# Householder QR in front of a transformer block: the column products move from VectorE to TensorE, one matmul per row chunk

## The chip, the cores and the metric

One Trainium2 chip, one of its cores. The metric is the device time of one launch in microseconds (us). The core's engines are called by the profile's names: PE is TensorE (PEld its weight loads), DVE is VectorE, ACT is ScalarE, POOL is GpSimd, SP issues DMAs. Each engine works through its own queue in order; they meet only at semaphores. Everything is float32.

## The reference, cut to what matters

The input `x` is 8 x 512 x 576, `cond` is 8 x 576. First the tokens are rotated inside a 64-dimensional subspace, and then a transformer block with modulation from `cond` runs over them:

```python
U, _ = jnp.linalg.qr(P)                       # P is 576 x 64
R = expm(skew(silu(cond) @ W.T + b))          # 8 rotations, 64 x 64
z = jnp.einsum('btn,nd->btd', x, U)
x = x + jnp.einsum('btd,nd->btn', einsum('btd,bde->bte', z, R) - z, U)
ada = silu(cond) @ ada_w + ada_b              # shift, scale, gate, twice
x = x + gate_msa * attention(modulate(layernorm(x)))   # per token, 16 x 16 over heads
x = x + gate_mlp * mlp(modulate(layernorm(x)))
```

The QR factorisation is needed before the first token can be rotated, and it is the part that is changed.

## The kernel before, in words

**Two stages.** The first 241 us hold the preparation: the QR, the exponentials and the modulation. From there to the end PE works through the transformer block for 8 batches in 16 units of 256 tokens (qkv, projection, fc1, fc2), while DVE does the attention of a later unit. The block begins with the rotation of the first 128 tokens, which needs the finished QR and the finished exponential of batch 0.

**The QR.** `m` holds P as five chunks of 128 rows (the last half empty): `[128, 5, 64]`. `qr_step(j)` is called for j = 0..63 in order; each step needs what the step before wrote to `m`. In the kernel before, one step with n = 64 - j columns left does this:

- DVE multiplies all chunks by column j (`pr`, L263) and adds the five chunks up (`t`, L268). From 16 columns on, both go in two halves of the columns. `column_products` does it at the end of the step before.
- PE fetches row j of `m` to all partitions (`rp`, L274, the weights are one column of the identity spread over 128 columns) and adds `t` over the partitions (`dp`, L282, the weights are ones). `dp[:, j]` is the squared norm, `dp[:, j+1:]` the products of column j with the others.
- DVE takes the sign (`sg`, L291), clears entry j of the column (L292), makes the signed row (`row`, L295); ACT takes the root (`nrm`, L298) and the negated sign (`nsg`, L299).
- DVE makes `w` (L320), `den` (L323), its reciprocal `r` (L335), the outer product (`up`, L327, two halves) and adds it to `m` with `r` (L337, two halves).
- `av`, `vmax`, `dg` (L306 to L310) and the write of the diagonal entry (L311, by `done`, in the next step) stand behind the products of the next column.

**The side work.** After each step from j = 2 on, one piece of `beside()` is put into the queues: the 40 matmuls that make the skew entries (L405), the nine column groups of `ada` (L364, five matmuls each, 128 x 8 weights, 384 columns), four modulation pieces (L375, weights 8 x 128) and the matrix exponential: products of 64 x 64 (L429, eight per product, 16 instructions), 13 pieces ahead of 19 squarings. A squaring makes two products (`pe`, `pf`), each copied by ACT and raised by POOL before the next squaring. `paced(4, ...)` lets four skew matmuls through per step, `paced(3, ...)` three modulation pieces, the latter also beside the first 13 pieces of the exponential. So j = 4 to 13 have skew matmuls, j = 14 to 30 `ada` and the start of the exponential, j = 31 to 49 the squarings, and j = 50 to 63 next to nothing.

**What sets the order.** PE, DVE, ACT and POOL carry their instructions in the order of the program here (a hand-written schedule); only the SP queue is ordered by the scheduler. So the order in which the loop calls `qr_step` and `beside` is the order of the queues. A float32 matmul is two LDWEIGHTS and two MATMUL instructions on PE; the profile counts both.

**After the loop** the diagonal entry of the last column is written (`done`), `vv` = the products of all columns (L577) gives the triangular inverse in some 30 us of small matmuls, and the rotation of the first tokens follows.

Of the kernel before, what the change touches and what calls it, by code (L numbers as in the profile page):

```python
# [18 lines left out]
R = 64  # L19
# [4 lines left out]
NK = len(KROWS)  # L24
# [25 lines left out]
def rotate_then_dit_block(  # L50
# [18 lines left out]
    nc = tc.nc  # L69
# [21 lines left out]
    ident = const.tile([128, 128], F32, tag="ident", name="ident")  # L91
# [23 lines left out]
    small = ctx.enter_context(tc.tile_pool(name="small", bufs=4))  # L115
# [48 lines left out]
    with tc.manual_schedule(engines=engines), tc.tile_pool(name="prep", bufs=1) as prep, tc.tile_pool(name="qrs", bufs=2) as qrs, tc.tile_pool(  # L164
        name="ada", bufs=4
    ) as adap, tc.tile_pool(name="exs", bufs=1) as exs, tc.tile_pool(
        name="ps_qr", bufs=1, space=PSUM
    ) as ps_qr, tc.tile_pool(
        name="ps_ex", bufs=2, space=PSUM
    ) as ps_ex, tc.tile_pool(name="ps_m", bufs=2, space=PSUM) as ps_m, tc.tile_pool(  # L170
        name="ps_x", bufs=1, space=PSUM
    ) as ps_x:
        m = prep.tile([128, NK, R], F32, tag="m", name="m")
# [12 lines left out]
        ones = prep.tile([128, 128], F32, tag="ones", name="ones")  # L186
# [56 lines left out]

        vmax = prep.tile([128, R], F32, tag="vmax", name="vmax")

        def halves(lo):
            n = R - lo
            if n < 16:  # L250
                return [(lo, R)]
            return [(lo, lo + n // 2), (lo + n // 2, R)]

        def wide(n):
            return [128, NK, n]

        def column_products(j):

            t = qrs.tile([128, R], F32, tag="t", name=f"t_{j}")
            prods = []  # L260
            for h, (a, b) in enumerate(halves(j)):
                pr = qrs.tile(wide(R), F32, tag=f"pr{h}", name=f"pr_{j}_{h}", bufs=1)
                nc.vector.tensor_tensor(  # L263
                    pr[:, :, a:b], m[:, :, a:b], m[:, :, j : j + 1].to_broadcast(wide(b - a)), ALU.mult
                )
                prods.append(pr)
            for pr, (a, b) in zip(prods, halves(j)):
                nc.vector.tensor_reduce(t[:, a:b], pr[:, :, a:b].rearrange("p c i -> p i c"), AX.X, ALU.add)  # L268
            return t

        def qr_step(j, t, done):

            rp = ps_qr.tile([128, R], F32, tag="rp", name=f"rp_{j}")
            nc.tensor.matmul(  # L274
                rp[:, j:R],
                lhsT=ident[:, j : j + 1].to_broadcast([128, 128]),
                rhs=m[:, 0, j:R],
                start=True,
                stop=True,
            )  # L280
            dp = ps_qr.tile([128, R], F32, tag="dp", name=f"dp_{j}")
            nc.tensor.matmul(dp[:, j:R], lhsT=ones, rhs=t[:, j:R], start=True, stop=True)  # L282

            def small(tag):
                return qrs.tile([128, 1], F32, tag=tag, name=f"{tag}_{j}")

            n = R - j
            row, sg, nsg, nrm, av = (small(x) if x != "row" else None for x in ("row", "sg", "nsg", "nrm", "av"))
            row = qrs.tile([128, R], F32, tag="row", name=f"row_{j}")

            nc.vector.tensor_scalar(sg, rp[:, j : j + 1], 0.0, -2.0, ALU.is_ge, ALU.mult)  # L291
            nc.vector.tensor_tensor(  # L292
                m[:, 0, j:R], m[:, 0, j:R], off[:, j : j + 1].to_broadcast([128, n]), ALU.mult
            )
            nc.vector.scalar_tensor_tensor(  # L295
                row[:, j:R], sg.to_broadcast([128, n]), 1.0, rp[:, j:R], ALU.add, ALU.mult
            )
            nc.scalar.activation(nrm, dp[:, j : j + 1], AF.Sqrt, bias=tiny)  # L298
            nc.scalar.activation(nsg, sg, AF.Identity, bias=ones[:, 0:1])  # L299
            if done:  # L300
                done()

            def finish():

                dg = small("dg")
                nc.vector.tensor_scalar(av, nrm, row[:, j : j + 1], None, ALU.subtract)  # L306
                nc.vector.tensor_reduce(
                    vmax[:, j : j + 1], m[:, :, j], AX.X, ALU.max, apply_absolute_value=True
                )
                nc.vector.tensor_scalar(dg, ident[:, j : j + 1], av, nsg, ALU.mult, ALU.mult)  # L310
                return lambda: nc.vector.tensor_tensor(  # L311
                    m[:, 0, j : j + 1], m[:, 0, j : j + 1], dg, ALU.subtract
                )

            if j + 1 == R:
                return None, finish()

            w = qrs.tile([128, R], F32, tag="w", name=f"w_{j}")
            den, r = small("den"), small("r")
            nc.vector.scalar_tensor_tensor(  # L320
                w[:, j + 1 : R], row[:, j + 1 : R], nrm, dp[:, j + 1 : R], ALU.mult, ALU.subtract
            )
            nc.vector.tensor_scalar(den, nrm, row[:, j : j + 1], nrm, ALU.subtract, ALU.mult)  # L323
            outer = []
            for h, (a, b) in enumerate(halves(j + 1)):
                up = qrs.tile(wide(R), F32, tag=f"up{h}", name=f"up_{j}_{h}", bufs=1)
                nc.vector.tensor_tensor(  # L327
                    up[:, :, a:b],
                    m[:, :, j : j + 1].to_broadcast(wide(b - a)),
                    w[:, a:b].unsqueeze(1).to_broadcast(wide(b - a)),  # L330
                    ALU.mult,
                )
                outer.append(up)
                if h == 0:
                    nc.vector.reciprocal(r, den)  # L335
            for up, (a, b) in zip(outer, halves(j + 1)):
                nc.vector.scalar_tensor_tensor(  # L337
                    m[:, :, a:b], up[:, :, a:b], r, m[:, :, a:b], ALU.mult, ALU.add
                )
            return column_products(j + 1), finish()  # L340

        def paced(n, parts):

            k = 0
            for part in parts:
                for _ in part:
                    k += 1
                    if k % n == 0:
                        yield
# [49 lines left out]
        def skew_entries(g):  # L399

            ps = ps_m.tile([B, GROUP], F32, tag="m", name=f"skew_{g}")
            cols = slice(g * GROUP, (g + 1) * GROUP)
            for c in range(NK):
                k = srows(c)
                nc.tensor.matmul(ps, lhsT=sc[0:k, c, :], rhs=wr[0:k, c, cols], start=c == 0, stop=c == NK - 1)  # L405
                yield
            nc.scalar.mul(skew[:, 1 + g * GROUP : 1 + (g + 1) * GROUP], ps, 2.0**-N_SQUARINGS)
# [109 lines left out]
        def modulations():  # L517

            for g in range(9):
                yield from ada_columns(g)  # L520
                if g + 4 < 9:
                    load_ada(g + 4)
                v = {1: 0, 2: 1, 5: 3, 7: 4}.get(g)
                if v is not None:
                    modulation(v)
                    yield

        def beside():
            yield
            yield  # L530
            yield from paced(4, [skew_entries(g) for g in range(8)])
            skew_rows()
            rest = paced(3, [modulations()])
            for _ in range(4):
                next(rest)
                yield
            for free in expm(*eyes):
                if free:
                    next(rest, None)
                yield  # L540
# [10 lines left out]
        first_xt = xin.tile([128, D], F32, tag="xt", name="xt_0_0", bufs=2)  # L551
        eyes = identities()
        side = beside()
        t, done = column_products(0), None
        for j in range(R):
            t, done = qr_step(j, t, done)
            if j > 1:
                next(side, None)
            if j == 30:
                nc.sync.dma_start(out=first_xT, in_=x_t[0, :, :, 0:256].rearrange("c p s -> p c s"))  # L560
                nc.sync.dma_start(out=first_xt, in_=x[0, 0:128, :])
            if j == 8:
                load_rows(wqkv, qkv_w, 65)
                nc.sync.dma_start(out=b1, in_=fc1_b)
# [4 lines left out]


        if True:
            done()
# [108 lines left out]
            for n in range(2):  # L681
                cols = slice(n * HALF, (n + 1) * HALF)
# [10 lines left out]
            for n in range(2):  # L693
# [513 lines left out]
    for k, (b, ts) in enumerate(units):  # L1207
# [5 lines left out]
        pr = Projection(b, ts, gate_a)  # L1213
# [89 lines left out]
```

## Time and profile before

| | us |
|---|---|
| median of three runs | 2156.08 (2156.01 to 2163.45) |
| profiled execution, its own time | 2157.38 |
| its span, first to last instruction | 2155.7 |
| QR, first `rp` to the end of the last `dp` | 4.51 to 209.42 |
| triangular inverse and first rotation | 209.4 to about 241 |
| transformer block | 241 to the end |

The 64 steps in five stretches, by the starts of `rp` in the trace:

| steps | side work | from, to (us) | us | us per step |
|---|---|---|---|---|
| j = 0 to 3 | none | 4.51 to 20.70 | 16.2 | 4.0 |
| j = 4 to 13 | skew | 20.70 to 56.92 | 36.2 | 3.6 |
| j = 14 to 30 | `ada`, start of the exponential | 56.92 to 119.89 | 63.0 | 3.7 |
| j = 31 to 49 | squarings | 119.89 to 176.91 | 57.0 | 3.0 |
| j = 50 to 63 | next to none | 176.91 to 209.42 | 32.5 | 2.3 |

How to read the lines that are quoted further on: a line of the timeline has the start, the time from the first start to the last end, the engine, the line of the kernel, the operation, the tiles (out<-in), shapes and how many instructions were merged (x2 is one float32 matmul). `128*8` is the shape of the weights. The view by windows gives, for a stretch of time, the busy time and the count of instructions of each engine, and PEclk, the share of its full clock that PE was granted. A busy time over the whole window is cut at the window's length.

### The profile page before, as it was taken

How to read it: one execution, taken by the hardware profiler on the slowest of the kernel's cores; microseconds unless marked ns; L12 is line 12 of the kernel's file. 1: busy time of each engine (PE TensorE's matmuls, PEld its weight loads, DVE VectorE, ACT ScalarE, POOL GpSimd, SP SyncE). 2: the span in 40 equal slices, each digit the busy share in tenths (PEclk: the TensorE clock that was granted, in tenths of full speed). 3: DMA queues.
4: the chain of work that ended last, by engine and by line, in shares of the span. 5: the costliest groups of instructions: out<-in, count | busy, mean ns of one | idle time of the engine just before them, and what ended most of it. 6: DMA issues, size and time to landing. Idle time of an engine off the chain costs nothing.

```text
span 2155.7 us, 28203 instructions
## 1 busy us (share of the span) xinstructions
PE 2052.0 (95%) x10091; PEld 1622.7 (75%) x10091; DVE 1818.0 (84%) x2544; ACT 433.6 (20%) x1040; POOL 731.8 (34%) x959
## 2 busy tenths in 40 slices
PE   6996998999999999999999999999999999999988
PEld 3475666777878888787878787888878778787867
DVE  8998499799997988979797979797988998986920
ACT  2232121212111111221121212111221121112110
POOL 2341143241523333333333242423333443343422
PEclk9965799999999999999999999999999999999989
DMA  8202265385857666565758484857667666665744
GB/s 278 87 2 75 85 209 164 114 234 161 225 178 223 194 191 222 174 217 178 234 143 271 133 266 127 244 176 210 213 180 234 187 210 182 200 189 193 218 129 131
DMA packets 251456, 392.44 MB, mean 182 GB/s; under 512 B 86926, under 2 KB 139099, under 8 KB 251316
## 3 DMA queue, kind: packets, MB, share of 16 engines
q1 hardware_dynamic: 225396, 364.09, 55.3%
q10 hardware_dynamic: 25920, 26.55, 3.6%
q8 instruction: 80, 1.31, 0.2%
q14 instruction: 60, 0.49, 0.1%
HBM read 331.63 MB, written 58.94 MB: 181 GB/s over the span
## 4 chain that ended last, share of the span: by engine, by line
PE 77%; DVE 12%; issue 3%; DMA 3%; POOL 3%; ACT 1%; ACTq 0%; SPq 0%; POOLq 0%; DVEq 0%
PE fc L993 25%; PE qkvp L821 17%; PE fc L1067 9%; PE pj L949 6%; PE fc L1072 6%; PE p L1097 3%; PE fc L1069 3%; DVE sc L866 2%; DVE qk L859 1%; DVE pv L887 1%; PE zps L751 1%; DVE att L894 1%; PE rot L762 1%; PE dp L282 1%; PE htr L794 1%
## 5 line engine op out<-in xcount | busy, mean ns | idle before, releaser
L993 PE MATMUL fc<-h2T,w 128*128 128x256 f32 x2304 | 521.1, 382 | 3.3 <-ACT h2T L969 2.1
L821 PE MATMUL qkvp<-wqkv,hT 128*128 128x288 f32 (+1 forms) x1920 | 486.5, 410 | 8.6 <-ACT qs L832 6.4
L993 PEld LDWEIGHTS fc<-h2T,w 128*128 128x128 f32 x2304 | 434.7, 191 | 71.7 <-ACT h2T L969 9.1
L821 PEld LDWEIGHTS qkvp<-wqkv,hT 128*128 128x128 f32 (+1 forms) x1920 | 364.3, 192 | 111.4 <-ACT qs L832 8.2
L859 DVE TENSOR_TENSOR qk<-qkv 128x2304 f32<-128x2304 f32 x128 | 336.8, 2631 | 15.3 <-DMA qkv<-tok 11.1
L887 DVE TENSOR_TENSOR pv<-sc,qkv 128x2304 f32<-128x2304 f32 x128 | 332.5, 2598 | 2.7
L894 DVE TENSOR_REDUCE att<-pv 128x144 f32<-128x2304 f32 x128 | 325.9, 2546 | 3.1
L866 DVE TENSOR_REDUCE sc<-qk 128x64 f32<-128x2304 f32 x128 | 326.0, 2547 | 2.5
L1092 POOL TENSOR_TENSOR s<-gt 128x128 f32<-128x128 f32 x144 | 93.5, 651 | 461.8 <-ACT gt L1014 461.8
L1014 ACT ACTIVATE gt<-fc,b 128x256 f32<-128x256 f32 x288 | 118.9, 472 | 604.5 <-PE fc L993 570.1
L1067 PE MATMUL fc<-wq,gt 128*128 128x288 f32 x576 | 170.5, 416 | 10.1 <-ACT gt L1014 7.5
L1072 PEld LDWEIGHTS fc<-wt,ss 128*128 128x128 f32 x1152 | 160.6, 190 | 15.1
L1072 PE MATMUL fc<-wt,ss 128*128 128x144 f32 x1152 | 164.7, 286 | 0.0
L832 ACT COPY qs<-qkvp 128x288 f32<-128x288 f32 x180 | 71.7, 398 | 377.0 <-PE qkvp L821 325.0
L1025 POOL TENSOR_TENSOR x<-x,mt 128x288 f32<-128x288 f32 x64 | 71.3, 1114 | 221.7 <-DVE mt L1024 221.7
L1089 POOL TENSOR_TENSOR ss<-gt 128x128 f32<-128x128 f32 x144 | 121.1, 841 | 65.1 <-PE fc L1072 65.0
L1091 POOL TENSOR_TENSOR ss<-gt,ss 128x128 f32<-128x128 f32 x144 | 130.5, 907 | 10.0
L1067 PEld LDWEIGHTS fc<-wq,gt 128*128 128x128 f32 x576 | 99.4, 190 | 44.5 <-issue 15.9
L949 PE MATMUL pj<-w2q_p,aT 128*128 128x288 f32 x384 | 105.2, 410 | 0.8 <-DVE u L1117 0.8
L146 POOL TENSOR_TENSOR rstd_m<-rstd_m,mhalf 128x1 f32<-128x1 f32 x32 | 24.5, 764 | 224.5 <-DVE rstd_m L145 224.5
L1067 PE MATMUL fc<-wt,gt 128*128 128x288 f32 x288 | 93.5, 406 | 0.0
L1069 PE MATMUL fc<-wq,ss 128*128 128x288 f32 x288 | 93.4, 406 | 0.0
(262 smaller groups left out, 2371.5 us busy)
## 6 DMA issues: line engine op xcount, KB each, us to landing
w<-in_fc_w SPq DMA_DIRECT2D x288, 256.0 KB, 5.0
wq<-in_fc_q SPq DMA_DIRECT2D x144, 432.0 KB, 4.3
wt<-comb_d SPq DMA_DIRECT2D x144, 432.0 KB, 5.9
tok<-qs ACTq DMA_DIRECT2D x180, 144.0 KB, 1.8
qkv<-tok SPq DMA_DIRECT2D x30, 864.0 KB, 4.6
w2q_p<-in_proj_w SPq DMA_DIRECT2D x32, 432.0 KB, 4.1
xT<-in_x_t SPq DMA_DIRECT2D x16, 640.0 KB, 4.8
w1t<-in_fc_t SPq DMA_DIRECT2D x80, 128.0 KB, 4.4
```

Source lines behind the costliest of these rows:

```text
L821: nc.tensor.matmul(ps, lhsT=hT[0:k, c, i * 128 : (i + 1) * 128], rhs=wqkv[0:k, c, cols], start=c == 0, stop=c == NK - 1,)
L859: nc.vector.tensor_tensor(pr, q[:, c * HC : (c + 1) * HC].unsqueeze(2).to_broadcast([128, HC, H, DH]), k.unsqueeze(1).to_broadcast([128, H ...
L866: nc.vector.tensor_reduce(sc[t][:, c * HC : (c + 1) * HC, :], pr, AX.X, ALU.add)
L887: nc.vector.tensor_tensor(pr, sc[t][:, c * HC : (c + 1) * HC, :].unsqueeze(2).to_broadcast([128, HC, DH, H]), v.unsqueeze(1).to_broadcast( ...
L894: nc.vector.tensor_reduce(att[:, c * HC : (c + 1) * HC, :], pr, AX.X, ALU.add)
L949: nc.tensor.matmul(ps, lhsT=aT[0:k, c, :], rhs=w, start=c == 0, stop=c == NK - 1)
L993: nc.tensor.matmul(bank[:, k], lhsT=lhs, rhs=h2T[rows, c, 0 : NU * 128], start=start, stop=stop, skip_group_check=True)
L1067: nc.tensor.matmul(p[k], lhsT=whole[k][0], rhs=whole[k][1], start=g == 0, stop=stop)
L1069: nc.tensor.matmul(p[2], lhsT=whole[2][0], rhs=whole[2][1], start=g == 0, stop=stop)
L1072: nc.tensor.matmul(bank[:, side], lhsT=lhs, rhs=rhs[:, n * QUARTER : (n + 1) * QUARTER], start=False, stop=stop, skip_group_check=True,)
L1089: nc.gpsimd.tensor_tensor(ss[:, 0], gt[:, 0, 1], gt[:, 1, 1], ALU.add)
L1091: nc.gpsimd.tensor_tensor(ss[:, 2], gt[:, 1, 0], ss[:, 1], ALU.subtract)
```

## The change

- `column_products` is gone. `dp` is now made by five matmuls that add up in PSUM: for chunk c the weights are column j of the chunk, spread over 128 columns, and the moving operand is the chunk's columns j to 63. `rp` stands behind the first of them.
- The update of `m` goes chunk by chunk: DVE first scales column j by `r` (`vr`, 128 x 5), then one instruction per chunk adds `w` times the chunk's entry of `vr`. The matmul of chunk c for the next step can start when chunk c is updated. The two halves and the `up` tiles are gone.
- `av` and `dg` leave the step: ACT keeps `nrm - row_j` and the negated sign in columns of `avs` and `nsgs`, and three instructions on DVE after the loop write all 64 diagonal entries.
- The side work is spread: two skew matmuls per step (j = 4 to 23), then two modulation pieces per step (j = 24 to 28), then the exponential from j = 29 with one or two pieces beside every step of it, the squarings at j = 42 to 60.

```diff
-        def column_products(j):
-            t = qrs.tile([128, R], F32, tag="t", name=f"t_{j}")
-            prods = []
-            for h, (a, b) in enumerate(halves(j)):
-                pr = qrs.tile(wide(R), F32, tag=f"pr{h}", name=f"pr_{j}_{h}", bufs=1)
-                nc.vector.tensor_tensor(
-                    pr[:, :, a:b], m[:, :, a:b], m[:, :, j : j + 1].to_broadcast(wide(b - a)), ALU.mult
...
-        def qr_step(j, t, done):
...
-            dp = ps_qr.tile([128, R], F32, tag="dp", name=f"dp_{j}")
-            nc.tensor.matmul(dp[:, j:R], lhsT=ones, rhs=t[:, j:R], start=True, stop=True)
+        avs = prep.tile([128, R], F32, tag="avs", name="avs")
+        nsgs = prep.tile([128, R], F32, tag="nsgs", name="nsgs")
+        def qr_step(j):
+            dp = ps_qr.tile([128, R], F32, tag="dp", name=f"dp_{j}")
+            rp = ps_qr.tile([128, R], F32, tag="rp", name=f"rp_{j}")
+            for c in range(NK):
+                nc.tensor.matmul(
+                    dp[:, j:R],
+                    lhsT=m[:, c, j : j + 1].to_broadcast([128, 128]),
+                    rhs=m[:, c, j:R],
+                    start=c == 0,
+                    stop=c == NK - 1,
                 )
+                if c == 0:
+                    nc.tensor.matmul(
+                        rp[:, j:R],
+                        lhsT=ident[:, j : j + 1].to_broadcast([128, 128]),
+                        rhs=m[:, 0, j:R],
+                        start=True,
+                        stop=True,
+                    )
...
+            nc.vector.tensor_reduce(vmax[:, j : j + 1], m[:, :, j], AX.X, ALU.max, apply_absolute_value=True)
             nc.scalar.activation(nrm, dp[:, j : j + 1], AF.Sqrt, bias=tiny)
-            nc.scalar.activation(nsg, sg, AF.Identity, bias=ones[:, 0:1])
...
+            nc.scalar.activation(avs[:, j : j + 1], row[:, j : j + 1], AF.Identity, bias=nrm, scale=-1.0)
+            nc.scalar.activation(nsgs[:, j : j + 1], sg, AF.Identity, bias=ones[:, 0:1])
...
-            for up, (a, b) in zip(outer, halves(j + 1)):
-                nc.vector.scalar_tensor_tensor(
-                    m[:, :, a:b], up[:, :, a:b], r, m[:, :, a:b], ALU.mult, ALU.add
-                )
-            return column_products(j + 1), finish()
+            nc.vector.reciprocal(r, den)
+            nc.vector.tensor_scalar(vr, m[:, :, j], r, None, ALU.mult)
+            for c in range(NK):
+                cols = m[:, c, j + 1 : R]
+                nc.vector.scalar_tensor_tensor(cols, w[:, j + 1 : R], vr[:, c : c + 1], cols, ALU.mult, ALU.add)
...
         def beside():
             yield
             yield
-            yield from paced(4, [skew_entries(g) for g in range(8)])
+            yield from paced(2, [skew_entries(g) for g in range(8)])
             skew_rows()
-            rest = paced(3, [modulations()])
-            for _ in range(4):
+            rest = modulations()
+            for _ in range(5):
+                next(rest)
                 next(rest)
                 yield
-            for free in expm(*eyes):
-                if free:
+            for k, free in enumerate(expm(*eyes)):
+                for _ in range(2 if free and k % 2 else 1):
                     next(rest, None)
                 yield
...
-            done()
+            dg = prep.tile([128, R], F32, tag="dg", name="dg")
+            nc.vector.tensor_tensor(dg, avs, nsgs, ALU.mult)
+            nc.vector.tensor_tensor(dg, dg, ident[:, 0:R], ALU.mult)
+            nc.vector.tensor_tensor(m[:, 0, :], m[:, 0, :], dg, ALU.subtract)
```

More of the change, by code (lines that the diff above doesn't have):

```diff
@@ L246, in rotate_then_dit_block @@
         vmax = prep.tile([128, R], F32, tag="vmax", name="vmax")
[L248 to L255, printed above, removed]
-        def column_products(j):
-            t = qrs.tile([128, R], F32, tag="t", name=f"t_{j}")
-            prods = []
-            for h, (a, b) in enumerate(halves(j)):
-                pr = qrs.tile(wide(R), F32, tag=f"pr{h}", name=f"pr_{j}_{h}", bufs=1)
-                nc.vector.tensor_tensor(
-                    pr[:, :, a:b], m[:, :, a:b], m[:, :, j : j + 1].to_broadcast(wide(b - a)), ALU.mult
-                )
[L266 to L269, printed above, removed]
@@ L271, in qr_step @@
-        def qr_step(j, t, done):
[L273 to L279, printed above, removed]
-            )
-            dp = ps_qr.tile([128, R], F32, tag="dp", name=f"dp_{j}")
[L282 to L291, printed above, removed]
+        avs = prep.tile([128, R], F32, tag="avs", name="avs")
@@ new lines, in rotate_then_dit_block, with small @@
+        nsgs = prep.tile([128, R], F32, tag="nsgs", name="nsgs")
[9 more added lines that the diff above has]
+                    stop=c == NK - 1,
+                )
+                if c == 0:
[6 more added lines that the diff above has]
+                    )
+            def small(tag, n=1):
+                return qrs.tile([128, n], F32, tag=tag, name=f"{tag}_{j}")
+            n = R - j
+            row, sg, nrm = small("row", R), small("sg"), small("nrm")
+            nc.vector.tensor_scalar(sg, rp[:, j : j + 1], 0.0, -2.0, ALU.is_ge, ALU.mult)
+            nc.vector.scalar_tensor_tensor(
+                row[:, j:R], sg.to_broadcast([128, n]), 1.0, rp[:, j:R], ALU.add, ALU.mult
+            )
@@ L294, in qr_step @@
             )
-            nc.vector.scalar_tensor_tensor(
-                row[:, j:R], sg.to_broadcast([128, n]), 1.0, rp[:, j:R], ALU.add, ALU.mult
-            )
+            nc.vector.tensor_reduce(vmax[:, j : j + 1], m[:, :, j], AX.X, ALU.max, apply_absolute_value=True)
             nc.scalar.activation(nrm, dp[:, j : j + 1], AF.Sqrt, bias=tiny)
-            nc.scalar.activation(nsg, sg, AF.Identity, bias=ones[:, 0:1])
-            if done:
-                done()
[L303 to L313, printed above, removed]
+            nc.scalar.activation(avs[:, j : j + 1], row[:, j : j + 1], AF.Identity, bias=nrm, scale=-1.0)
+            nc.scalar.activation(nsgs[:, j : j + 1], sg, AF.Identity, bias=ones[:, 0:1])
             if j + 1 == R:
-                return None, finish()
-            w = qrs.tile([128, R], F32, tag="w", name=f"w_{j}")
-            den, r = small("den"), small("r")
+                return
+            w, den, r, vr = small("w", R), small("den"), small("r"), small("vr", NK)
+            nc.vector.tensor_scalar(den, nrm, row[:, j : j + 1], nrm, ALU.subtract, ALU.mult)
             nc.vector.scalar_tensor_tensor(
@@ L322, in qr_step @@
             )
[L323 to L335, printed above, removed]
-            for up, (a, b) in zip(outer, halves(j + 1)):
-                nc.vector.scalar_tensor_tensor(
-                    m[:, :, a:b], up[:, :, a:b], r, m[:, :, a:b], ALU.mult, ALU.add
-                )
-            return column_products(j + 1), finish()
+            nc.vector.reciprocal(r, den)
[3 more added lines that the diff above has]
+                nc.vector.scalar_tensor_tensor(cols, w[:, j + 1 : R], vr[:, c : c + 1], cols, ALU.mult, ALU.add)
         def paced(n, parts):
@@ L553, in rotate_then_dit_block @@
         side = beside()
-        t, done = column_products(0), None
         for j in range(R):
-            t, done = qr_step(j, t, done)
+            qr_step(j)
             if j > 1:
@@ L571, in rotate_then_dit_block @@
         if True:
-            done()
+            dg = prep.tile([128, R], F32, tag="dg", name="dg")
+            nc.vector.tensor_tensor(dg, avs, nsgs, ALU.mult)
+            nc.vector.tensor_tensor(dg, dg, ident[:, 0:R], ALU.mult)
+            nc.vector.tensor_tensor(m[:, 0, :], m[:, 0, :], dg, ALU.subtract)
             below = ps_ex.tile([R, 1], F32, tag="ex", name="below")
```

## The prediction

> **What bounds the kernel now.** I read the page first. PE is busy nearly throughout, and granted its full clock except in slices 3 to 5 (108 to 270 us) and one near the end. The change touches the first four.
>
> ```profile
> span 2155.7 us, 28203 instructions
> ...
> PE   6996998999999999999999999999999999999988
> ...
> PEclk9965799999999999999999999999999999999989
> ```
>
> Nothing of the transformer block can start before the QR ends, so a microsecond in the QR is taken as a microsecond of the whole. Next I asked the chain of waits what ends the steps: between 60 and 70 us it is mostly DVE work (`t`, `m`, `pr`, `up`), but between 140 and 150 us, in the squarings, it is PE alone, `pe`, `pf`, `rp`, `dp`:
>
> ```profile
> by line: PE pf L429 37.0%; PE pe L429 29.6%; PE dp L282 19.3%; PE rp L274 16.6%
> ```
>
> So the late steps are already bound by PE, the engine that the change loads. Then the timeline of all engines in step j = 2, early, with PE slow. The reader is to see the order `dp`, root, `w`, `den`, `r`, update, and the gaps: 0.04 us from `dp` to the root, 0.03 from an end to a dependent start.
>
> ```profile
> 14.34 0.66 PE L282 MATMUL dp<-t,ones 128*128 128x62 f32 x2 [0.55 <-DVE av L306]
> ...
> 15.04 0.26 ACT L298 ACTIVATE nrm<-dp,tiny 128x1 f32<-128x1 f32 x1 [3.45 <-PE dp L282]
> ...
> 15.33 0.28 DVE L320 SCALAR_TENSOR_TENSOR w<-row,nrm,dp 128x61 f32<-128x61 f32 x1 [0.24 <-ACT nrm L298]
> 15.53 0.27 DVE L323 TENSOR_SCALAR den<-nrm,row 128x1 f32<-128x1 f32 x1
> ...
> 16.22 0.66 DVE L337 SCALAR_TENSOR_TENSOR m<-up,r,m 128x150 f32<-128x150 f32 x2
> ```
>
> Then PE's own timeline, for the price of a matmul with 128 weight columns and few moving columns, at both clocks:
>
> ```profile
> 22.46 3.53 PE L405 MATMUL skew<-wr,sc 128*8 128x252 f32 x8
> 25.92 0.68 PE L274 MATMUL rp<-m,ident 128*128 128x59 f32 x2
> 26.39 0.64 PE L282 MATMUL dp<-t,ones 128*128 128x59 f32 x2
> ...
> 31.24 1.87 PE L405 MATMUL skew<-wr,sc 128*8 128x252 f32 x8
> ```
> ```profile
> 85.65 0.42 PE L274 MATMUL rp<-m,ident 128*128 128x42 f32 x2
> 85.89 0.40 PE L282 MATMUL dp<-t,ones 128*128 128x42 f32 x2
> ```
> ```profile
> 236.59 2.50 PE L751 MATMUL zps<-xT,u 128*128 128x128 f32 x10
> ```
>
> From `rp` to `dp` is 0.47 us slow and 0.24 fast; the same eight skew instructions take 3.53 and 1.87. Five matmuls in a row (`zps`) take 2.50 slow. At half clock such a matmul costs 0.45 us however few columns move, at full clock 0.24, and the last one needs 0.64 or 0.40 to its end.
>
> Last the view by windows, cut as the clock changes, every 3.41 us from 30.95 us on (before that the record has no clock; the durations say half).
>
> ```profile
> 24.12:27.53 3.41, 3.41 (x11) 1.56 (x10) 2.44 (x13) 0.44 (x2) 0.00 (x0) 1.00 1.07 373
> 34.36:37.77 3.41, 2.61 (x12) 1.19 (x13) 3.32 (x19) 0.81 (x3) 0.00 (x0) 1.00 1.06 385
> ...
> 92.39:95.80 3.41, 2.80 (x12) 1.30 (x12) 3.32 (x18) 0.91 (x3) 3.07 (x5) 1.00 0.35 129
> 95.80:99.21 3.41, 3.41 (x16) 2.58 (x17) 2.67 (x14) 0.70 (x4) 3.07 (x5) 0.50 0.00 0
> ...
> 147.00:150.41 3.41, 3.41 (x50) 3.24 (x50) 3.37 (x24) 1.37 (x5) 1.41 (x2) 0.50 0.00 0
> ```
>
> Being busy is not what raises the clock: at 147 us PE is busy in all of 3.41 us, with 3.24 us of weight loads, and stays at half clock. What fits is the time in which moving columns stream, N columns taking 2N/2400 us per instruction at full clock (252 columns: 0.21 of the 0.23 seen) and twice that at half, an instruction with 64 rows counted half. Worked out so, the windows that kept the full clock had 44% or more (34.36: 52%), those that lost it 39% or less (92.39). From half clock 74% (24.12) and the squarings' 50 to 69% did not raise it, 84% and more did (78.7, 99.2, 235.8 us). Weight loads don't count. That is an estimate from this trace.
>
> **The change part by part.** One step at half clock, prices as above: five distances of 0.45 and 0.64 for the last `dp` make 2.89; root 0.04 + 0.26; `den` 0.03 later; `w` 0.19 behind it, `r` 0.20 behind `w` and 0.15 long, `vr` 0.03 + 0.20 (as `av`, one scalar operand), first chunk update 0.03 + 0.27 (not in the trace; between `row`'s 0.21 and the 0.37 of a 155-column L337, nearest to `w`'s 0.28). From there to the first matmul 0.12, as from `t` to `dp`. Sum 4.4 us, 4.2 with few columns. The other four updates, some 0.2 us apart, hide behind the matmuls (0.45 apart), and `sg`, `row`, `off`, `vmax` behind the rest; gone are `pr`, `t`, `up`, `av`, `dg`, some 1.9 us of DVE in step 2. If that cover were thin (full clock), the updates come 0.2 apart against 0.24: still PE. At full clock the step is 5 x 0.24 + 0.40 + the same 1.5 = 3.1, late 3.0.
>
> PE's queue is in order, so side work stands between `dp` and the next `rp`; a step takes at least 6 x 0.45 = 2.70 (full: 1.44) plus that. Prices from the same timeline, half/full: skew instruction 0.44/0.23, an `ada` matmul 1.30/0.68 (six instructions 4.01 at 98.26, 2.10 at 102.96), sixteen 64 x 64 instructions 1.0/0.53 (32 in 1.9 to 2.0 at 147; 0.52 apart at 105.86), a modulation piece 2.1/1.2 (seven instructions 1.55 at 95.67, ten 1.26 at 68.73) and, before it, 1.2 for its ACT copy, which now stands behind root and the two ACT instructions of the step.
>
> All at half clock: j = 0 to 3, 4 x 4.4 = 17.6. j = 4 to 23, 2.70 + 4 x 0.44 = 4.46, x 20 = 89.2. j = 24 to 28, 2.70 + 2.6 = 5.3, x 5 = 26.5. j = 29 to 41: four with a product and two `ada` 6.3, one with two `ada` 5.3, one with two products 6.0, two modulation pieces 6.3, five hidden in 4.3: 70.6. Squarings, 2.70 + 2.0 + 1.3 = 6.0, x 16, two with a modulation piece 6.8, the last 5.0: 114.6. j = 61 to 63: 11.2. Sum 330 against 204.9: +125. At full clock from j = 4: 17.6 + 62.6 + 15.5 + 43.1 + 61.6 + 7.7 = 208: +3.
>
> Which clock? Skew steps at half clock stream 12 x 0.10 + 4 x 0.42 us, less a little for 65-row chunks, in 4.46 us: 62%, in the densest window 70 to 73%: below 74, so half. The early modulation and exponential steps reach 80% only where a window falls on the `ada` burst, and drop again (one `ada` a step is 30% at full clock). In the squarings `pe`, `pf`, `ada` make 3.3 us at 86%; a window that falls on them, about one step in five, raises the clock, and then 48% a window holds it until a modulation piece. I take 11 steps at full clock, each 6.0 - 3.3 = 2.7 less: -30.
>
> Side effects: three DVE instructions for the diagonal and the ACT one before them, about 1.55 us from last `dp` to `vv` against 1.18: +0.4. SP: `gates_d` and the last `ada` loads come later, with the weight prefetch behind them, at the QR's end; before, DMA runs at 0.09 of its share in 209 to 241 us, so I cost it at nothing; uncovered, it is some 5 us. Exponential: its last product comes at j = 60, two steps ahead of need. Sum 125 - 30 + 0.4 = +95; on the profiled 2157.4 that is 2252, on the median, 1.3 lower, 2251.
>
> A rule against my reading stands in the Trainium skill, TensorE: Matmul & The Clock Gate, section Why this matters for your kernels: keep TensorE busy for 4 us or more without a break and it gets past the warm-up window to full clock. By it, a PE that is busy without a break from j = 4 on runs at full clock, and the sum is +3. The row at 147 us has PE busy without a break at half clock, so I keep the row.
>
> **The rivals.** (1) Half clock throughout, +125, 2281: the squaring burst must fit a 3.41 us window almost exactly, and if 64 x 64 products count a quarter, never does. (2) Full clock from j = 4, +3, 2160, no measurable change (0.5%, 10.8 us, is about what a measurement can tell): for it speaks that PE has no pauses; against it 147.00. (3) Full clock for skew and early steps, half from the squarings on: 57 + 3, 2216. (4) Faster: full clock, and the DVE part 0.25 us shorter than my 1.5 in each of 64 steps: 3 - 16 = -13, 2144; it takes over 0.2 us a step to matter, and the row prices leave no such slack.
>
> **How the numbers follow.** Mostly half clock, 2225 to 2275: 0.55. (1) 0.2, (3) 0.13, (2) 0.08, (4) 0.04. The range 2185 to 2290 leaves out (2), (4) and a little beyond both ends. Slower by over 0.5%: 0.88.
>
> **What would show it.** PEclk 0.5 over most of 5 to 300 us; `dp` to `dp` distances of 0.45; steps j = 4 to 23 near 4.4 us; squarings near 6.0 with spells of 3.3; the chain of waits PE nearly throughout; `vv` at about 300 us instead of 210.60. It is wrong if PEclk is 1.0 in the skew steps (the weight loads would count after all), or if matmuls with spread weights come closer than 0.43 us at half clock.

## The result, and the profile after

The change makes the kernel slower: a median of 2233.69 us (2229.73 to 2237.66) against 2156.05, ratio 1.0353 with a 95% interval of 1.0335 to 1.0371. The forecast was 2251 in a range of 2185 to 2290. It was right on the side and on the reason (half clock), and 17 us too high.

The QR now ends at 286.81 us instead of 209.42, 77.4 us later, against 77.6 us between the medians: the loss is in the QR. By the starts of the first matmul of each step:

| steps of the changed kernel | predicted (us) | measured (us) |
|---|---|---|
| j = 0 to 3 | 17.6 | 17.6 |
| j = 4 to 23, skew | 89.2 | 90.2 |
| j = 24 to 41, modulation and start of the exponential | 26.5 + 70.6 | 19.9 + 55.4 |
| j = 42 to 60, squarings | 114.6 - 30 | 88.7 |
| j = 61 to 63 | 11.2 | 10.8 |
| sum (before: 204.9) | 299.7 | 282.5 |

The page of the changed kernel, its span, PE's busy tenths and the granted clock in slices of 55.8 us:

```profile
span 2230.4 us, 28909 instructions
...
PE   8999989899999999999999999999999999999988
...
PEclk9985869999999999999999999999999999999989
```

PE is busy as before. The clock record has no event before 122.7 us, so the first two nines say nothing; the durations below show the half clock. The chain of waits between 60 and 70 us, where DVE's work ended the steps of the kernel before:

```profile
by line: PE dp L257 54.7%; PE skew L367 40.7%; PE rp L265 8.5%
```

Now all of it is PE. The timeline of step j = 4 shows why: start, time from the first start to the last end, engine, line, tiles.

```profile
21.90 0.65 PE L257 MATMUL dp<-m 128*128 128x60 f32 x2 [1.59 <-DVE m L302]
22.35 0.63 PE L265 MATMUL rp<-m,ident 128*128 128x60 f32 x2
22.78 1.92 PE L257 MATMUL dp<-m 128*128 128x60 f32 x8
24.62 1.85 PE L367 MATMUL skew<-wr,sc 128*8 128x252 f32 x4
24.73 0.26 ACT L287 ACTIVATE nrm<-dp,tiny 128x1 f32<-128x1 f32 x1 [3.61 <-PE dp L257]
25.85 1.04 DVE L302 SCALAR_TENSOR_TENSOR m<-w,vr,m 128x59 f32<-128x59 f32 x5
26.40 0.68 PE L257 MATMUL dp<-m 128*128 128x59 f32 x2
```

The matmuls with 128 weight columns come 0.45 us apart (21.90, 22.35, 22.78), four skew instructions take 1.8, and the step is 26.40 - 21.90 = 4.50 us. Each of DVE's five updates is done before PE wants it: they begin at 25.85, while PE is still in the skew work, and are all done at 26.89, while PE, from 26.40 on, takes one chunk every 0.45 us. The first clock event is a raise in j = 24 to 41, where the view by windows was cut along the clock's steps:

```profile
119.17:122.58 3.41, 3.41 (x9) 1.29 (x9) 1.75 (x10) 0.74 (x3) 0.00 (x0) 1.00 0.00 0
122.70:126.11 3.41, 3.25 (x20) 1.98 (x19) 2.02 (x12) 1.18 (x4) 0.00 (x0) 1.00 0.00 0
132.93:136.34 3.41, 2.95 (x26) 2.77 (x25) 2.39 (x15) 1.34 (x6) 0.00 (x0) 1.00 0.81 262
...
221.57:224.98 3.41, 3.41 (x34) 2.01 (x30) 1.39 (x9) 1.07 (x4) 1.40 (x2) 0.50 0.00 0
```

Columns: window, its length, busy time and instruction count of PE, PEld, DVE, ACT and POOL, then PEclk. In 119.17 to 122.58 PE has only nine instructions, and four of them, the `ada` ones of 384 columns, fill the window from 120.16 us on (2.4 of the 3.41 us); in the next window PE does 20, at full clock. It stays so until 136.3, and comes back three times before j = 42: together 34 of the 75 us of that stretch at full clock. A step at full clock in that stretch (j = 27, from 125.85 to 128.89 us) has two `ada` matmuls, four instructions:

```profile
126.29 1.06 PE L257 MATMUL dp<-m 128*128 128x37 f32 x8
127.28 1.46 PE L326 MATMUL ada<-aw,sc 128*8 128x384 f32 x4
128.89 0.38 PE L257 MATMUL dp<-m 128*128 128x36 f32 x2 [0.15 <-DVE m L302]
```

In the squarings the clock is full from 225.1 to 259.2. The timeline there, first a step at half clock, then one at full clock:

```profile
203.13 0.83 DVE L302 SCALAR_TENSOR_TENSOR m<-w,vr,m 128x19 f32<-128x19 f32 x5
204.07 0.72 POOL L475 TENSOR_TENSOR ex_e<-ex_e,ex_i 128x256 f32<-128x256 f32 x1 [4.56 <-PE pf L391]
204.75 0.72 POOL L475 TENSOR_TENSOR ex_f<-ex_f,ex_i 128x256 f32<-128x256 f32 x1
...
230.74 0.81 PE L326 MATMUL ada<-aw,sc 128*8 128x384 f32 x2
230.85 1.83 DVE L302 SCALAR_TENSOR_TENSOR m<-w,vr,m 128x14 f32<-128x14 f32 x5
230.96 0.72 POOL L475 TENSOR_TENSOR ex_f<-ex_f,ex_i 128x256 f32<-128x256 f32 x1 [2.16 <-PE pe L391]
231.48 0.39 PE L257 MATMUL dp<-m 128*128 128x14 f32 x2
231.65 0.72 POOL L475 TENSOR_TENSOR ex_e<-ex_e,ex_i 128x256 f32<-128x256 f32 x1
...
232.45 0.74 PEld L257 LDWEIGHTS dp<-m 128*128 128x128 f32 x6 [0.23 <-DVE m L302]
```

At half clock POOL's two additions of a squaring begin after the five updates, which take 0.83 us. At full clock the products end sooner, the additions fall on the updates, and the same five take 1.83 us although they have fewer columns. PE takes the first chunk of the next step straight after its `ada` matmul (231.48), but the weights of the third chunk wait 0.23 us for its update; nothing of that was in the forecast.

### The profile page after: what moved, and what is told of

Same layout as the page of the kernel before. It is cut to its first block, busy times and chain, and to the rows that moved or that the text cites. A ratio compares the mean times of both kernels' runs of the same rounds, so it can differ in the third digit from the quotient of the medians.

```text
span 2230.4 us, 28909 instructions
## 1 busy us (share of the span) xinstructions
PE 2152.1 (96%) x10603; PEld 1703.6 (76%) x10603; DVE 1786.4 (80%) x2285; ACT 449.3 (20%) x1104; POOL 729.0 (33%) x959
## 4 chain that ended last, share of the span: by engine, by line
PE 74%; DVE 15%; issue 4%; POOL 3%; DMA 2%; ACT 2%; ACTq 0%; SPq 0%; POOLq 0%; DVEq 0%
PE fc L958 23%; PE qkvp L786 14%; PE fc L1032 8%; PE dp L257 5%; PE fc L1037 5%; PE pj L914 5%; DVE sc L831 3%; DVE qk L824 3%; PE fc L1034 3%; PE p L1062 2%; DVE att L859 2%; DVE pv L852 2%; PE skew L367 2%; PE ada L326 1%; PE zps L716 1%
## 5 line engine op out<-in xcount | busy, mean ns | idle before, releaser
L257 PEld LDWEIGHTS dp<-m 128*128 128x128 f32 x640 | 126.4, 281 | 67.1 <-ACT nsgs L289 26.1
L257 PE MATMUL dp<-m 128*128 128x64 f32 (+58 forms) x640 | 139.7, 358 | 15.9 <-DVE m L302 9.7
L1056 POOL TENSOR_TENSOR ss<-gt,ss 128x128 f32<-128x128 f32 x144 | 141.5, 983 | 10.0
L1054 POOL TENSOR_TENSOR ss<-gt 128x128 f32<-128x128 f32 x144 | 116.2, 807 | 67.4 <-PE fc L1037 67.3
```

The source lines that it names most:

```text
L257: nc.tensor.matmul(dp[:, j:R], lhsT=m[:, c, j : j + 1].to_broadcast([128, 128]), rhs=m[:, c, j:R], start=c == 0, stop=c == NK - 1,)
L1056: nc.gpsimd.tensor_tensor(ss[:, 2], gt[:, 1, 0], ss[:, 1], ALU.subtract)
```

## The experiments

Theory: the step's five chunk matmuls make PE the bound at half clock, and it is the clock, not the number of matmuls, that carries the loss. Rivals: the new order of the side work is the cause; or the five matmuls are too many at any clock. Ratios are against the kernel before on the same chip, with 95% intervals.

**The new steps with the old order of the side work.**

```diff
-            yield from paced(2, [skew_entries(g) for g in range(8)])
+            yield from paced(4, [skew_entries(g) for g in range(8)])
...
-            rest = modulations()
-            for _ in range(5):
-                next(rest)
+            rest = paced(3, [modulations()])
+            for _ in range(4):
                 next(rest)
                 yield
...
```

> The new steps with the side work paced as before (four skew matmuls or three modulation pieces a step, squarings at j = 31 to 49). Theory (the matmuls per chunk cost PE time, most of it at half clock): 17.6 for j = 0 to 3, about 38 for the ten skew steps (the dense skew bursts raise the clock), 68 for 17 steps with modulation, 19 squaring steps of 4.7 at half clock = 89, 14 bare steps of 4.2 = 59: 272 us of QR, some 67 more than before, time about 2223. Rival (the loss comes from spreading the side work into the squarings): within 10 us of before, 2156 to 2166.

Measured: 2237.95, ratio 1.0357 (1.0327 to 1.0386). So the steps alone make the loss, 79 us against the kernel before. With the same side work beside the same steps, the two kernels can now be laid side by side:

| steps | before (us) | new steps (us) | difference | clock of the new steps |
|---|---|---|---|---|
| j = 0 to 3 | 16.2 | 17.7 | +1.5 | half |
| j = 4 to 13 | 36.2 | 35.5 | -0.7 | full from 28.0 us |
| j = 14 to 30 | 63.0 | 83.8 | +21 | changing |
| j = 31 to 49, squarings | 57.0 | 84.3 | +27 | half from 147.5 us |
| j = 50 to 63 | 32.5 | 57.0 | +25 | half |

The differences add up to some 74 of the 79 us; the rest lies behind the QR, where the full clock came back 39 us after its end (321.6 us), in the kernel before 30 us after it (239.2 us).

A skew step there, with four skew matmuls per step, holds the full clock; PE's timeline:

```profile
31.46 0.43 PE L257 MATMUL dp<-m 128*128 128x58 f32 x2
31.73 0.39 PE L265 MATMUL rp<-m,ident 128*128 128x58 f32 x2
31.95 1.06 PE L257 MATMUL dp<-m 128*128 128x58 f32 x8
32.94 1.87 PE L367 MATMUL skew<-wr,sc 128*8 128x252 f32 x8
34.74 0.43 PE L257 MATMUL dp<-m 128*128 128x57 f32 x2
```

34.74 - 31.46 is 3.28 us, with twice the skew work of the changed kernel's 4.50-us step. At full clock the new step is no slower than the old one (3.4 to 3.3 us in the same place). The late steps have no side work and take 4.2 us at half clock, against 2.3 to 2.5 of the old steps.

**The old steps with the new order of the side work**, the mirror of the edit above, put into the kernel before.

```diff
-            yield from paced(4, [skew_entries(g) for g in range(8)])
+            yield from paced(2, [skew_entries(g) for g in range(8)])
...
```

> The steps of before with the side work spread as after. Theory: PE has two or three weight loads a step less to fit and the step stays bound by DVE, but at half clock; skew steps 3.5, squaring steps 3.0 to 4.2: 5 to 30 us above before, 2161 to 2186. Rival (the spreading is the cause): 2220 and above.

Measured: 2171.97, ratio 1.0056 (1.0033 to 1.0079), the QR at 221.1 us. The new order costs some 12 us with the old steps: with two skew matmuls per step the clock stays at half until 94.6 us. With the new steps it costs nothing: the changed kernel has a ratio of 1.0353 with it, 1.0357 without.

**The changed kernel with filler matmuls.** A filler has 8 weight columns and up to 512 moving columns of ones, and its product is not used. It stands behind the side work and fills the step up to a given number of moving columns (64-row instructions counted half).

```diff
+            while n >= 32:
+                k = min(n, 512)
+                nc.tensor.matmul(wps[:, 0:k], lhsT=fill[:, 0:8], rhs=fill[:, 0:k], start=True, stop=True)
+                n -= k
...
+            streamed[0] += 6 * (R - j)
+            fill_up(2048 if j == 0 else 1050 if j < 42 else 900)
```

> After, with matmuls of 8 weight columns and up to 512 moving columns of ones, never read, put behind each step's side work, so that each step streams about 1050 columns (900 from j = 42). Nothing else changes. Theory (the clock follows the streaming, and the half clock costs most of the loss): PEclk 1.00 from about 10 us on, skew steps 3.1 to 3.2, squarings about 3.6, QR about 215 us, time 2163 to 2172, although PE does more work. Rival (PE is not held by its clock but by its weight loads or by waits): PEclk or the steps stay as in after and the added matmuls lengthen them: 2234 to 2300.

Measured: 2191.91, ratio 1.0135 (1.0107 to 1.0164), between the two forecasts. Steps j = 4 to 23 fell from 4.5 to 3.1, but the clock was lost from 117.8 to 145.1 and from 175.8 to 203.1 us, in steps with a modulation piece (short matmuls with few columns). So more columns, and 512 ahead of each modulation piece:

```diff
+            fill_up(2048 if j == 0 else 1050 if j < 24 else 1250 if j < 42 else 1050)
...
+            before_mod()
             ps = ps_m.tile([128, NK, B], F32, tag="m", name=f"mod_{v}")
```

> After with stronger filling: 1050 columns a step to j = 23, 1250 to j = 41, 1050 from there, and 512 ahead of each modulation piece, where PE waits for ACT. The first filled kernel lost the full clock at 117.8 and 175.8 us in the steps with a modulation piece. Theory (clock): full clock from about 12 us to the end of the QR, squaring steps 3.4 to 3.8, QR 222 to 228 us, time 2172 to 2180, some 55 below after. Rival (weight loads and waits hold PE, not its clock): no step below those of after in the stretches where the clock was half before, 2220 or more.

Measured: 2178.31, ratio 1.0076 (1.0050 to 1.0102): the loss falls from 3.5% to 0.8%, with more work for PE than in the changed kernel. PE's timeline of a skew step, and then the same 30 us of both kernels in the view by windows, the changed kernel first:

```profile
39.90 0.39 PE L283 MATMUL rp<-m,ident 128*128 128x54 f32 x2
40.12 1.06 PE L275 MATMUL dp<-m 128*128 128x54 f32 x8
41.11 1.02 PE L387 MATMUL skew<-wr,sc 128*8 128x252 f32 x4
41.97 0.54 PE L219 MATMUL wps<-fill 128*8 128x222 f32 x2
42.76 0.40 PE L275 MATMUL dp<-m 128*128 128x53 f32 x2 [0.25 <-DVE m L320]
```
```profile
30.00:60.00 30.00, 30.00 (x109) 20.11 (x107) 16.59 (x90) 5.47 (x22) 0.00 (x0) 1.00 0.62 205
```
```profile
30.00:60.00 30.00, 28.34 (x178) 18.44 (x177) 23.33 (x126) 7.71 (x31) 0.00 (x0) 1.00 0.63 208
```

With the filler PE does 178 matmul instructions in the time of 109 and even waits for DVE (0.25 us). (The changed kernel's 1.00 stands only for a clock that has no record yet.) Half a microsecond of useless streaming buys 1.4 us a step. What is left of the loss lies from j = 24 on, where steps at full clock still take 3.3 to 5.1 us and the clock was lost for two windows (105.7 and 122.8 us). The QR ended at 230.3 us, so it took 21 us longer than in the kernel before.

**The price of the five matmuls.** Only chunk 0's matmul is made; the products of the other four chunks are left out of the computation.

```diff
-            for c in range(NK):
+            for c in range(1):
                 nc.tensor.matmul(
...
```

> After with only the first chunk's matmul of dp; the products of the other four chunks are left out of the computation. DVE, ACT and the side work are unchanged. Theory (the four matmuls of PE time are the price): PE part of a step 0.9 instead of 2.7 at half clock, steps j = 0 to 3 about 2.6, skew steps 2.7, cold squaring steps 4.2, QR 200 to 225 us, 58 to 82 below after, time 2152 to 2176. Rival (the chain root, den, w, r, vr, update on DVE and ACT sets the step): the steps stay above 4 us, at most 15 us below after, 2219 to 2234.

Measured: 2161.76, ratio 0.9998 (0.9985 to 1.0010): 72 us below the changed kernel, and no slower than the kernel before. Without the four chunk matmuls nothing is left of the loss, although the clock is again at half up to 81.3 us. The steps took 3.0 to 2.9 rather than the 2.7 forecast at j = 4 to 23. From the timeline of such a step, at half clock like the changed kernel:

```profile
40.74 0.64 PE L257 MATMUL dp<-m 128*128 128x52 f32 x2
41.17 0.63 PE L265 MATMUL rp<-m,ident 128*128 128x52 f32 x2
41.73 1.85 PE L367 MATMUL skew<-wr,sc 128*8 128x252 f32 x4
...
43.71 0.64 PE L257 MATMUL dp<-m 128*128 128x51 f32 x2
```

The step takes 43.71 - 40.74 = 2.97 us: PE works for some 2.7 of them (two matmuls at 0.45 and 1.8 of skew) and waits for the first update. The old step took 3.7 to 3.3 beside the same side work at half clock (the experiment before the fillers), so VectorE's part did become shorter; the four matmuls take more than that.

**The diagonal entries alone**, in the kernel before: `av` and `dg` leave the step, three instructions after the loop write all entries.

```diff
-            nc.scalar.activation(nsg, sg, AF.Identity, bias=ones[:, 0:1])
-            if done:
-                done()
+            nc.scalar.activation(avs[:, j : j + 1], row[:, j : j + 1], AF.Identity, bias=nrm, scale=-1.0)
+            nc.scalar.activation(nsgs[:, j : j + 1], sg, AF.Identity, bias=ones[:, 0:1])
...
```

> Before with one part of the change alone: the diagonal entries are kept in avs and nsgs and written after the loop, av, dg and the write leave DVE's step. Theory: these three stand where DVE waits for dp and the root (0.8 us a step), or PE sets the step; nothing moves, 2154 to 2160. Rival (DVE's own work sets the step): 0.4 us a step less, 64 x 0.4 = 26 us, about 2131.

Measured: 2162.74, ratio 1.0000 (0.9986 to 1.0014). This part of the change is worth nothing that the times show. (In the profiled execution the QR ended 3.7 us earlier, at 205.8 us; the clock was raised earlier there too, at 25.7 instead of 31.0 us, so how much of it is the diagonal's is open.)

**Does the kernel before gain from the full clock?** It loses the clock at 123.1 us for the rest of the QR, so fillers might help it too.

```diff
+            streamed[0] += 2 * (R - j)
+            fill_up(2048 if j == 0 else 1000 if j < 31 else 760 if j < 50 else 640)
```

> Before, with the same kind of filling matmuls (1000 columns a step to j = 30, 760 in the squarings, 640 after). Theory: full clock also in the squarings, which were bound by PE at 3.0 a step and fall to about 2.7, and shorter dp waits in the first four and the last steps: 5 to 15 us less than before, 2141 to 2151. Rival (before is bound by DVE and by the copies of the squarings whatever the clock): 2153 to 2160.

Measured: 2185.97, ratio 1.0116 (1.0092 to 1.0140), a miss: the clock was lost for good at 122.1 us, and the fillers, slow themselves, lengthened every squaring step to 3.6. With more columns, and 512 ahead of each modulation piece:

```diff
+            fill_up(2048 if j == 0 else 1100 if j < 14 else 1250 if j < 31 else 1050 if j < 50 else 850)
```

> Before with stronger filling (1100, 1250, 1050 and 850 columns a step in the four stretches, 512 ahead of modulation pieces). The first filled kernel of before lost the clock at 122 us for good, and its fillers then made each squaring step 0.7 longer. Theory: full clock from about 10 us to the end of the QR, squaring steps 2.7 to 2.9 instead of 2.93, last steps about 2.2 instead of 2.4: 0 to 8 us less than before, 2148 to 2157. Rival (DVE and the copies bound the steps at either clock, and the fillers are in the way): 2160 to 2180.

Measured: 2166.72, ratio 1.0019 (1.0003 to 1.0035), a miss again, though the clock was now full from 9.8 to 221.4 us. The squaring steps took 3.6 to 3.8, longer than 2.91 at half clock. In them POOL's additions stood beside DVE's large instructions. Two kernels tell this from simply too much filler. Both are the kernel before with the diagonals at the end, no filler in j < 4, and some 330 columns in the squaring steps; the first has them behind the two products of a squaring, the second ahead of them, and that is the only difference (the last line only resets the count):

```diff
+            if squarings:
+                fill_up(900 - 8 * R)
             if j > 1:
                 next(side, None)
             if squarings:
-                streamed[0] -= 8 * R
-                fill_up(900 - 8 * R)
+                streamed[0] = 0
```

> Kernel before with the diagonals at the end and filler matmuls from j = 4 on, in the squaring steps (j = 31 to 49) some 330 columns behind the two products of a squaring. With fillers at full clock the squaring steps took 3.6 to 3.8 us, longer than 2.91 at half clock. Theory A (POOL's two additions of a squaring, 0.72 us each, now fall on DVE's large instructions and stretch them: two L355 updates took 0.98 where they take 0.48, pr 0.90 instead of 0.36): the order is as there, so the steps stay near 3.5, some +11 us over 19 steps, time +1 to +4 us against before. Theory B (the 430 columns of filler were simply too much for PE): with a quarter less the steps fall to 2.9 or less, time 4 to 10 us below before.

> The same kernel with the same fillers; only in the squaring steps they stand ahead of the two products, so that the products, ACT's copies and POOL's additions come some 0.6 us later, beside the short DVE instructions instead of the updates. Theory A: updates and pr back to 0.48 and 0.36, squaring steps 2.5 to 2.8, time 6 to 12 us below before (0.994 to 0.997). Theory B: as in the kernel with the fillers behind, the two within 2 us of each other.

Measured: behind, 2163.80, ratio 1.0013 (1.0003 to 1.0023); ahead, 2145.54, ratio 0.9926 (0.9911 to 0.9941). The same matmuls in another order are worth 18 us. The timeline of a squaring step of each, the one with the fillers behind first:

```profile
140.19 0.48 DVE L350 SCALAR_TENSOR_TENSOR m<-up,r,m 128x65 f32<-128x65 f32 x2
140.20 0.73 PE L219 MATMUL wps<-fill 128*8 128x334 f32 x2
140.42 0.83 POOL L530 TENSOR_TENSOR ex_e<-ex_e,ex_i 128x256 f32<-128x256 f32 x1 [2.20 <-PE pf L445]
140.59 1.43 DVE L283 TENSOR_TENSOR pr<-m 128x65 f32<-128x65 f32 x2
141.22 0.72 POOL L530 TENSOR_TENSOR ex_f<-ex_f,ex_i 128x256 f32<-128x256 f32 x1
```
```profile
140.41 0.74 PE L219 MATMUL wps<-fill 128*8 128x340 f32 x2
140.50 0.72 POOL L530 TENSOR_TENSOR ex_f<-ex_f,ex_i 128x256 f32<-128x256 f32 x1
...
141.47 0.47 DVE L350 SCALAR_TENSOR_TENSOR m<-up,r,m 128x55 f32<-128x55 f32 x2
141.85 0.34 DVE L283 TENSOR_TENSOR pr<-m 128x55 f32<-128x55 f32 x2
142.38 0.73 POOL L530 TENSOR_TENSOR ex_f<-ex_f,ex_i 128x256 f32<-128x256 f32 x1 [1.17 <-PE pe L445]
```

Behind the products, the two `pr` of a step take 1.43 us beside POOL; with the fillers ahead, POOL is between its additions when DVE makes `m` and `pr`, and the two `pr` take 0.34 (this step has fewer columns; two of 65 columns take 0.35 in the kernel before, at 138.83 us, without POOL beside them). The additions now fall on the short instructions, of which only the clearing of entry j is slowed, to 0.48 us (142.67) from 0.17. Behind, most squaring steps took 3.5 to 3.9 us (up to 4.9 where the clock was lost as well, from 121.0 to 127.8 and 155.1 to 165.3 us); ahead, 2.8 to 2.5, and the QR ended at 194.2 us instead of 214.1. That last kernel's clock is full from 26.1 to 200.1 us, and it beats both kernels.

```profile
span 2144.1 us, 28291 instructions
...
PEclk9998999999999999999999999999999999999989
```

The squarings took 69.1 us behind and 49.0 ahead. Where the clock is full in both, at j = 37 to 40, the steps take 3.65 to 3.72 and 2.57 to 2.65 us: 1.07 us a step, which over 19 steps is already the whole difference. The two spells of lost clock in the first kernel, 6.8 and 10.2 us, add little to it.

## Why the prediction was right, and where it was off

- **The clock decides, and it is half.** Right. The skew steps came out at 4.51 (4.46 forecast), the steps without side work at 4.39 (4.4), `dp` to `dp` at 0.45. The rivals with full clock in the skew steps (2160, 2216 and 2144) are out, since the clock was at half there; half clock throughout (2281) is out by six spells of full clock before the QR's end, 72 us together. Filling the same steps up to the full clock took them to 3.1, the forecast price of a step at full clock without side work, here with two skew matmuls; DVE's 0.25 us of waiting shows that PE was no longer alone in setting it.
- **Busy is not streaming.** Confirmed by the pair of windows from 30 to 60 us: 30.00 us busy at half clock, 28.34 us busy at full clock, told apart by a filler of 222 columns. The time of weight loads doesn't tell them apart: the window at 24.12 us of the kernel before, with 1.56 us of them, did not raise the clock, the one at 221.57 here, with 2.01, did.
- **The four extra chunk matmuls are the price.** Right: leaving them out gives back the whole loss (ratio 0.9998), filling up to the full clock most of it (1.0076). So the matmuls make the loss, and the half clock sets most of what they cost. The 0.8% that is left near full clock was not taken apart: the fillers themselves, two lost windows and POOL's additions beside the updates are in it too.
- **Failed step: j = 24 to 41.** The text let the windows on the `ada` burst raise the clock "and drop again", and costed that at nothing (26.5 + 70.6). The clock was raised there four times and held for 34 us in all, and the stretch took 75.3 instead of 97.1: -22 us. The 30% for which the text let it drop again was worked out for one `ada` matmul a step, but the steps j = 24 to 28 have two. By the text's own estimate, four `ada` instructions of 0.32 us and twelve of 0.03 stream 1.64 of the 3.04 us of such a step at full clock, 54%, above the 44% that had held the clock; by windows it was 41 to 51% from 122.7 to 132.9 us. That stretch should have had a term of its own.
- **Squarings: -30 forecast, -26 measured.** The eleven full-clock steps at 3.3 were, by the trace, nine at 3.56 (j = 48 to 56), one in part (j = 57) and j = 60 at 2.98. The windows of the nine come out at 38 to 49%, where the text had 48 to hold the clock. The step named "still PE" the bound at full clock, with updates 0.2 us apart. Beside POOL's additions they are 0.37 apart (1.83 for five), and PE waits for the third: its six distances of 0.24 took 1.74 us (231.48 to 233.22) instead of 1.44, about the 0.26 by which the step exceeds 3.3.
- **Side effects.** The last `dp` to `vv` took 1.64 us (286.81 to 288.45) against 1.18, +0.5 as forecast (+0.4). The profiled executions differ by 74.7, 3 less than the QR; the executions of one kernel differ by more than that (2152.84 to 2163.45 for the one before).

With -21.8, +4.1 on the squarings, +1.0 on the skew steps and -0.4 on the last ones, the forecast's 299.7 becomes the measured 282.5 (rounded terms).

## What to carry to other kernels

Before work is moved to TensorE, work out its stream of moving columns, window by window, for the new step: matmuls of few columns with full-width weights keep the engine busy and hold its clock down, and then every matmul costs nearly double (0.45 instead of 0.24 us here). Where a step falls short, a matmul with few weight columns and many moving columns can be cheaper than the clock that it saves, but only if it is enough to hold it: in the kernel before, 1000 and then 760 columns a step lost the clock and 27 us, while 1100 to 1250 and then 1050, with 512 more ahead of the modulation pieces, held it. Holding it was not yet a gain there (2166.72 against 2162.86 us). Look too at what a faster engine pulls forward: the order of a filler and a product was worth 18 us here, because it decides what VectorE does while GpSimd adds, and only with the right order did the fillers gain (0.7% against the kernel before).

## What the runs showed of the hardware that was not expected

VectorE's instructions with two operands in SBUF are slowed by GpSimd's additions beside them: the five updates take 1.83 us with 14 columns instead of 0.83 with 19, a pair of `pr` of 65 columns 1.43 instead of 0.35, while the additions themselves stay at 0.72 to 0.83. The Trainium skill, SBUF — State Buffer, section Who interferes with whom, says that a VectorE instruction with two SBUF inputs contends with a GpSimd instruction that reads SBUF, and that the port pair they share is an exclusive lock. The runs agree. In the kernel with the fillers behind the products, a `pr` of 70 columns begins 0.04 us after an addition and ends 0.09 us after its end, 0.77 us long; in the kernel before, `pr` of 60 to 75 columns take 0.21 to 0.23 in the squarings:

```profile
137.51 0.72 POOL L530 TENSOR_TENSOR ex_e<-ex_e,ex_i 128x256 f32<-128x256 f32 x1
137.55 0.77 DVE L283 TENSOR_TENSOR pr<-m 128x70 f32<-128x70 f32 x1
```

The runs agree with the limit to two inputs as well: `vmax`, a reduction with one SBUF input, takes 0.15 us beside an addition (139.88 us in the last kernel) and 0.14 to 0.15 without.

The clock's bounds come out of the stream of moving columns, as estimated in the forecast, with each instruction's stream spread evenly over its recorded time. The clock changes at steps of 3.41 us, so the QR of every kernel here was cut into such windows. In the changed kernel, windows that kept the full clock stream 38 to 51%, windows that lost it 13 to 39%; windows that raised it 76 to 85% (221.7 us: 76), and none that stayed at half is above 74% (201.2 us). Over all twelve kernels, 779 windows, those that kept the clock have 37% or more and those that lost it 40% or less, those that raised it 73% or more and those that stayed at half 75% or less. So the bounds lie near 40% and near 75%. That is an estimate: putting an instruction's stream at the start or the end of its time moves single windows by some 4 points.
